# Three small-tile sums and one branch moved in a four-layer graph kernel

## The chip, the cores and the metric
One core of one Trainium2 chip runs the whole program. The metric is device microseconds of one execution; lower is better. Before the change: 2198.82 us, the median of 3 runs (2195.28 to 2202.48).

## The reference
2708 nodes with 256 features pass through four layers; each layer is an attention over an adjacency matrix (`gnn`) and then a feed-forward part (`ffn`), both added to x. Three of the eight parts are touched:

```python
# layer 0 ffn: soft assignment of every node to 64 slices per head, 8 heads
sw = softmax((xm @ W_slice.T + b_slice) / temp)       # 2708 x 512
st = einsum(fx, sw) / (sw.sum + 1e-5); ot = hydra(st) # small
x  = x + einsum(ot, sw) @ out_w.T + out_b
# layer 1 gnn
x  = x + concat([a @ n / deg, n]) @ weight + bias     # n = layernorm(x)
# layer 2 ffn ("mixture two"): 4 experts, two per node
g  = top-2 softmax of the scores, 0 for the other two experts
x  = x + sum over e of g[:, e] * (gelu(n @ W1[e] + b1[e]) @ W2[e] + b2[e])
```

All of it is float32.

## The kernel before
The 2708 nodes are 21 tiles of 128 and one of 20 (`NT` is 22), grouped in `CHUNKS`: five of 512 columns and one of 148, which is a tile of 128 and the tile of 20. Everything stays in the on-chip memory between layers; adjacency and weights stream in. The text is written in program order, and a scheduler then interleaves independent parts on each engine. A `tc.If(...)` block keeps its body together: each of the five engines reads the flag into a register (a tensor load), compares, and jumps over the body when the flag is zero. The scheduler may place instructions that stand outside the block before or behind it: TensorE does the first transposes of unit 0, written after `rare`, ahead of the branch, and SyncE does the flag reads of all three blocks one after the other.

**Slices** (`fast_l0_ffn`, L2481 to L2541). For each tile t TensorE forms the logits `lg` from two products (kk = 0, 1) that accumulate in one PSUM tile (L2482); VectorE adds the bias out of PSUM (L2494), takes a maximum per head (L2495), subtracts (L2496); ScalarE takes the exponential (L2499); VectorE sums (L2500), inverts (L2501) and multiplies (L2502). Then TensorE adds the tile into the four sums `T` (L2508) and transposes it (L2515). After the small middle part, four products accumulate in `po` for each tile (L2533), and VectorE adds `po` to x (L2541).

**Projections** (`fast_l1_gnn`). For each chunk the normalized rows are transposed (`ft_ps`, L1650), and each tile takes four products: two accumulate in `v`, two in `own` (L2605). ScalarE rounds `v` to the high part of V (L2613), VectorE forms the low part (L2614) and adds `own` to x (L2617). The 20 rows of the last tile are then copied by GpSimd's queue to four places (`Vf`, L1588). Behind these copies in the same queue stand the adjacency loads `at` (L2569, 256 KB each); eight buffers of them are filled ahead. The loop over the 21 full source tiles follows (L2646).

**Mixture two** (`fast_l2_ffn`). Expert 0 runs over all chunks and writes to `first` (`park`). `deal.rank` then makes lists of the nodes that use experts 1 and 2; GpSimd gathers these rows (L4581) into `xe`, of which three sets fit. `last_used` sets a flag, whether any node uses expert 3; here none does. Eight units follow, (chunk c, expert i) in turn: `turn` transposes the gathered rows (L4814) through one PSUM tile `xt_ps` in two groups (kk), each copied out by VectorE or ScalarE (L100, L101) before the next may start; `up` multiplies (L4650) and takes the gelu (L4657); `down` multiplies again (L4669), and VectorE adds the bias (L4859) before GpSimd scatters the rows (L4595). Chunk 0 and the last chunk of 148 nodes run plainly for experts 1 and 2 (`expert`, `add`: L4686, L4784), interleaved at the end with `steps`, the first part of layer 3's attention (L3744, L3781). `rare` (L4798) is the block with the branch, for expert 3: it stands once before the units, once after unit 1 and once after unit 2.

Where a tile has only 20 rows, `down` already uses another form: the four products of the sum go to four separate groups of 32 columns of TensorE's array (`y[32 * q : ...]`), each one started and stopped alone, and VectorE adds the four parts (`summed`, L4686 and L4688). It does so for every expert:

```python
g = 1 if n > 32 else 4
```

Of the kernel before, what the change touches and what calls it, by code (L numbers as in the profile page):

```python
# [2450 lines left out]
def fast_l0_ffn(k, w, front):  # L2451

    nc, tc = k.nc, k.tc
    ident = k.ident
    H, P, G = 8, 64, 64
    DI = H * P
    with ExitStack() as ctx:
        keep = ctx.enter_context(tc.tile_pool(name="b0", bufs=1))  # L2460
        swT = keep.tile([128, 4, N], F32, name="swT")
        Tn = keep.tile([128, 4, D + 1], F32, name="Tn")
        Z = keep.tile([128, 4, D], F32, name="Z")
        slices = Slices(k, w, ctx)
        fa, fT, wc, bw = front.fa, front.fT, front.wc, front.bw

        with tc.tile_pool(name="b0t", bufs=3) as tmp:
            with tc.tile_pool(name="ps_b0l", bufs=2, space=PSUM) as psl, tc.tile_pool(
                name="ps_b0T", bufs=1, space=PSUM
            ) as psT:  # L2470

                def psum():
                    return psl.tile([128, 512], F32, name="swt_ps")

                side = front.chunk(*CHUNKS[-1], psum)
                T = [psT.tile([128, D + 1], F32, name=f"T{q}_ps") for q in range(4)]
                for t in range(NT):
                    p = sz(t)
                    next(side, None)
                    lg = psl.tile([128, DI], F32, name="lg_ps")  # L2480
                    for kk in range(2):  # L2481
                        nc.tensor.matmul(  # L2482
                            lg[:p],
                            lhsT=fT[:, kk, t * 128 : t * 128 + p],
                            rhs=wc[:, kk, :],
                            start=(kk == 0),
                            stop=(kk == 1),
                        )
                    xt = k.x[:p, t, :]
                    nc.gpsimd.tensor_tensor(xt, xt, slices.ob[:p], ALU.add)  # L2490
                    sw = tmp.tile([128, DI], F32, name="sw")
                    mx = tmp.tile([128, H], F32, name="mx")
                    s3 = sw[:p].rearrange("p (h g) -> p h g", h=H)
                    nc.vector.tensor_tensor(sw[:p], lg[:p], bw[:p], ALU.add)  # L2494
                    nc.vector.tensor_reduce(mx[:p], s3, AX.X, ALU.max)  # L2495
                    nc.vector.tensor_tensor(  # L2496
                        s3, s3, mx[:p, :, None].to_broadcast([p, H, G]), ALU.subtract
                    )
                    nc.scalar.activation(sw[:p], sw[:p], AF.Exp)  # L2499
                    nc.vector.tensor_reduce(mx[:p], s3, AX.X, ALU.add)  # L2500
                    nc.vector.reciprocal(mx[:p], mx[:p])  # L2501
                    nc.vector.tensor_tensor(  # L2502
                        s3, s3, mx[:p, :, None].to_broadcast([p, H, G]), ALU.mult
                    )
                    tp = psum().rearrange("p (q n) -> p q n", q=4)
                    for q in range(4):
                        cols = slice(q * 128, (q + 1) * 128)
                        nc.tensor.matmul(  # L2508
                            T[q],
                            lhsT=sw[:p, cols],  # L2510
                            rhs=fa[:p, t, :],
                            start=(t == 0),
                            stop=(t == NT - 1),
                        )
                        end = nc.tensor.transpose(tp[:, q, :p], sw[:p, cols], ident[:p, :p])  # L2515
                    nc.scalar.copy(swT[:, :, t * 128 : t * 128 + p], tp[:, :, :p])
                k.busy(psl.tile([128, DI], F32, name="lg_ps"), 6, end)
                for q in range(4):
                    sc = tmp.tile([128, 1], F32, name="sc")
                    nc.vector.tensor_scalar(sc, T[q][:, D : D + 1], 1e-5, None, ALU.add)  # L2520
                    nc.vector.reciprocal(sc, sc)
                    if q < 3:
                        nc.scalar.activation(Tn[:, q, :], T[q], AF.Copy, scale=sc)
                    else:
                        nc.vector.tensor_scalar(Tn[:, q, :], T[q], sc, None, ALU.mult)

        slices.mix(Tn, Z)
        with tc.tile_pool(name="ps_b0o", bufs=3, space=PSUM) as ps:
            for t in range(NT):
                p = sz(t)  # L2530
                po = ps.tile([128, D], F32, name="o_ps")
                for q in range(4):
                    nc.tensor.matmul(  # L2533
                        po[:p],
                        lhsT=swT[:, q, t * 128 : t * 128 + p],
                        rhs=Z[:, q, :],
                        start=(q == 0),
                        stop=(q == 3),
                    )
                xt = k.x[:p, t, :]  # L2540
                nc.vector.tensor_tensor(xt, xt, po[:p], ALU.add)  # L2541


def fast_l1_gnn(k, adjT, weight, bias, order, after, other):
# [6 lines left out]
    with ExitStack() as ctx:  # L2551
# [25 lines left out]
        with tc.tile_pool(name="a1f", bufs=1) as pf, tc.tile_pool(  # L2577
            name="a1t", bufs=3
        ) as tmp, tc.tile_pool(name="a1c", bufs=2) as two, tc.tile_pool(
            name="ps_a1v", bufs=4, space=PSUM  # L2580
        ) as psv, tc.tile_pool(name="ps_ft", bufs=3, space=PSUM) as psf:
            w = pf.tile([128, 4, D], F32, name="w")
            nc.sync.dma_start(w, weight.rearrange("(k p) d -> p k d", p=128))
            b = pf.tile([128, D], F32, name="b")
            nc.sync.dma_start(b, brow(bias, D))

            for c0, cs in CHUNKS:
                bl = blocks(c0, cs)
                t0 = bl[0][0]
                fa = two.tile([128, 4, D], F32, name="fa")  # L2590
                fT = two.tile([128, 2, 512], F32, name="fT")
                for _ in k.norm_chunk(two, fa, t0, len(bl)):
                    pass
                k.transposed(
                    fa,
                    bl,
                    lambda: psf.tile([128, 512], F32, name="ft_ps"),
                    lambda kk: fT[:, kk, :cs],
                    t0,
                )  # L2600
                for t, c, p in bl:
                    v, own = [psv.tile([128, D], F32, name="v_ps") for _ in range(2)]
                    for half, o in enumerate((v, own)):
                        for kk in range(2):
                            nc.tensor.matmul(  # L2605
                                o[:p],
                                lhsT=fT[:, kk, c : c + p],
                                rhs=w[:, half * 2 + kk, :],
                                start=(kk == 0),
                                stop=(kk == 1),  # L2610
                            )
                    hi, lo = V[:p, t, :D], V[:p, t, D + 2 :]
                    nc.scalar.copy(hi, v[:p])  # L2613
                    nc.vector.tensor_tensor(lo, v[:p], hi.bitcast(F32), ALU.subtract)  # L2614
                    xt = k.x[:p, t, :]
                    nc.gpsimd.tensor_tensor(xt, xt, b[:p], ALU.add)
                    nc.vector.tensor_tensor(xt, xt, own[:p], ALU.add)  # L2617
# [1987 lines left out]
def fast_l2_ffn(k, w, edges, deal, then):  # L4605
# [7 lines left out]
    with ExitStack() as ctx:  # L4613
# [48 lines left out]
        def down(e, hT, bl, use):  # L4662
            for t, o, n in bl:
                y = ps2.tile([128, D], F32, name="y_ps")
                g = 1 if n > 32 else 4
                for m in range(M // g):
                    for q in range(g):
                        mq = m + q * M // g
# [15 lines left out]

        def summed(dst, y, n, e):
            done = nc.vector.tensor_tensor(dst, y[:n], b2[:n, e, :], ALU.add)  # L4686
            for q in range(1, 1 if n > 32 else 4):
                done = nc.vector.tensor_tensor(  # L4688
                    dst, dst, y[32 * q : 32 * q + n], ALU.add
                )  # L4690
            return done
# [105 lines left out]
        def rare(chunks):  # L4797
            with tc.If(nc.values_load(flag, min_val=0, max_val=1)):  # L4798
                for c0, cs in chunks:
                    expert(E - 1, c0, cs, add(E - 1))  # L4800

        rare(deal.C[:2])
        steps = then()
        pst = ctx.enter_context(tc.tile_pool(name="ps_mt", bufs=1, space=PSUM))
        zp = ctx.enter_context(tc.tile_pool(name="mz", bufs=2))
# [41 lines left out]
        for u, (c, i) in enumerate(units):  # L4847
# [14 lines left out]

            down(1 + i, hT, [(s, s * 128, 128) for s in range(deal.T[i])], use)
            xT = xT_next
            if u == 1:
                rare(deal.C[2:])
            if u == 2:
# [756 lines left out]
```

## Time and profile before
| what | value |
|---|---|
| runs | 2202.48, 2198.82, 2195.28 us |
| profiled execution, its own time | 2216.88 us |
| its span, first to last instruction | 2215.1 us |
| TensorE busy, matmul / weight load | 2124.0 us (96%) / 1455.6 us (66%) |
| VectorE, ScalarE, GpSimd busy | 1471.3, 887.0, 487.8 us |
| mean granted TensorE clock | 0.987 |
| slices, logits | 374 to 472 us |
| slices, output sums | 507 to 545 us |
| projections | 547 to 589 us |
| mixture two | about 1345 to 1606 us |

The profiled execution is 18.06 us longer than the median of the runs. In the profile PE is TensorE's matmul, PEld its weight load, DVE VectorE, ACT ScalarE, POOL GpSimd, SP SyncE; a `q` behind the name is that engine's instruction queue. Views by line give the time, the length, the instructions and, in brackets, how long the engine sat idle before it and what released it. A float32 product is two records on PE ("passes"), each with its own weight load.

### The profile page before, as it was taken

The numbers are of one execution on the slowest core, as the hardware profiler recorded it, in microseconds if no ns is written. First come the engines' busy times: TensorE is split into PE (matmuls) and PEld (weight loads), VectorE is DVE, ScalarE is ACT, GpSimd is POOL, SyncE is SP. The second block draws the span as 40 slices with busy tenths as digits, with TensorE's granted clock in tenths as the row PEclk, the third lists the DMA queues.
The fourth block names the chain that finished last, engine by engine and source line by source line (L and its number), as shares of the span: only waits on it lengthen the run. The fifth ranks groups of instructions, "written<-read, shape, count | busy, mean of one in ns | idle before, by whom it ended". The sixth has DMA issues, their size and how long they took to land. (4 is left out here: it accounts for less than half of the span.)

```text
span 2215.1 us, 31872 instructions
## 1 busy us (share of the span) xinstructions
PE 2124.0 (96%) x11415; PEld 1455.6 (66%) x11415; DVE 1471.3 (66%) x3190; ACT 887.0 (40%) x1798; POOL 487.8 (22%) x565
## 2 busy tenths in 40 slices
PE   9999999999999999999999999989999999999995
PEld 5766665557899677777678886657743333337784
DVE  7478887866596476755765655554678887885553
ACT  7655665231211322212251003223577777752221
POOL 3100002412354334665400010224110000003321
PEclk9999999999999999999999999999999999999998
DMA  5244432121399334243345554013133434335540
GB/s 163 59 113 115 115 87 90 38 81 47 109 252 257 96 72 122 55 96 79 58 152 144 149 168 117 13 44 97 43 83 105 115 96 116 106 106 165 166 140 14
DMA packets 164164, 234.87 MB, mean 106 GB/s; under 512 B 28556, under 2 KB 97522, under 8 KB 163987
## 3 DMA queue, kind: packets, MB, share of 16 engines
q1 hardware_dynamic: 110616, 156.09, 24.5%
q0 software_dynamic: 35712, 61.71, 11.2%
q10 hardware_dynamic: 17658, 14.81, 2.0%
q8 instruction: 99, 1.62, 0.3%
q14 instruction: 79, 0.64, 0.1%
HBM read 200.27 MB, written 32.77 MB: 105 GB/s over the span
## 5 line engine op out<-in xcount | busy, mean ns | idle before, releaser
L4068 PE MATMUL acc_ps<-PU,V 128*64 128x512 f32 (+5 forms) x1512 | 309.4, 547 | 0.4 <-DVE PU L3910 0.4
L3898 ACT ACTIVATE PU<-Rr,iQ 128x512 f32<-128x512 f32 (+2 forms) x378 | 222.1, 663 | 48.3 <-PE acc_ps L4068 47.4
L3860 DVE SCALAR_TENSOR_TENSOR PT<-Rr,Q,aj 128x512 f32<-128x512 f32 (+3 forms) x252 | 169.7, 683 | 99.1 <-PE acc_ps L3989 68.5
L4068 PE MATMUL acc_ps<-PT,V 128*64 128x512 f32 (+5 forms) x504 | 222.5, 549 | 0.1
L1910 PE MATMUL acc_ps<-fa,PT 128*128 128x257 f32 x882 | 215.6, 383 | 2.5 <-ACT out L1930 1.3
L1910 PEld LDWEIGHTS acc_ps<-fa,PT 128*128 128x128 f32 x882 | 163.7, 190 | 68.9 <-issue 36.2
L3910 DVE SCALAR_TENSOR_TENSOR PU<-PU,aj 128x1536 f32<-128x1536 f32 (+2 forms) x126 | 195.3, 1561 | 6.8 <-ACT PU L3898 6.7
L3989 PE MATMUL acc_ps<-V,PT 128*128 128x257 f32 x882 | 193.8, 381 | 0.0
L3989 PEld LDWEIGHTS acc_ps<-V,PT 128*128 128x128 f32 x882 | 166.3, 190 | 26.0 <-DVE PT L3860 0.8
L3476 PE MATMUL y_ps<-w2t,hT 128*128 128x256 f32 (+1 forms) x784 | 162.7, 387 | 4.1 <-PEq L3654 3.7
L3458 PE MATMUL h_ps<-xT,w1t 128*128 128x384 f32 (+2 forms) x544 | 163.4, 457 | 1.9 <-ACT hT L3465 1.3
L3476 PEld LDWEIGHTS y_ps<-w2t,hT 128*128 128x128 f32 (+1 forms) x784 | 132.4, 182 | 28.9 <-issue 6.4
L4068 PEld LDWEIGHTS acc_ps<-PU,V 128*64 128x64 f32 (+1 forms) x1512 | 91.4, 122 | 83.6 <-issue 72.0
L3465 ACT ACTIVATE hT<-h_ps,b1t 128x384 f32<-128x384 f32 (+2 forms) x136 | 73.2, 539 | 165.1 <-PE h_ps L3458 163.0
L3458 PEld LDWEIGHTS h_ps<-xT,w1t 128*128 128x128 f32 x544 | 101.9, 195 | 54.9 <-ACT hT L3465 3.2
L4068 PEld LDWEIGHTS acc_ps<-PT,V 128*64 128x64 f32 (+1 forms) x504 | 53.3, 122 | 115.9 <-issue 109.6
L2646 PE MATMUL acc_ps<-V,at 128*128 128x258 f32 (+3 forms) x924 | 120.1, 286 | 2.2 <-DMA at<-in_adjT 1.1
L1854 PE MATMUL s_ps<-KT,QT 128*128 128x512 f32 (+1 forms) x252 | 116.4, 549 | 2.5 <-POOL KT L1816 1.4
L1879 DVE SCALAR_TENSOR_TENSOR PT<-aj,PT 128x512 f32<-128x512 int32 (+1 forms) x126 | 79.8, 638 | 55.7 <-ACT PT L1878 55.5
L1834 ACT ACTIVATE junk<-aj,mhalf 128x512 bf16<-128x512 int32 (+1 forms) x126 | 84.3, 669 | 80.0 <-DMA aj<-in_adjT 79.2
L2646 PEld LDWEIGHTS acc_ps<-V,at 128*128 128x128 f32 (+1 forms) x924 | 112.0, 185 | 6.2 <-DMA at<-in_adjT 2.1
L3505 POOL DMA_INDIRECT acc<-ys,ids x45 | 92.9, 2064 | 101.0 <-DVE no L3652 28.8
(908 smaller groups left out, 3757.3 us busy)
## 6 DMA issues: line engine op xcount, KB each, us to landing
aj<-in_adjT SPq DMA_DIRECT2D x294, 256.0 KB
at<-in_adjT POOLq DMA_DIRECT2D x105, 256.0 KB
w1t<-in_L_ffn_W SPq DMA_DIRECT2D x8, 1024.0 KB
w2t<-in_L_ffn_W SPq DMA_DIRECT2D x8, 1024.0 KB
w1t<-in_L_ffn_w SPq DMA_DIRECT2D x8, 1024.0 KB
w2t<-in_L_ffn_w SPq DMA_DIRECT2D x8, 1024.0 KB
fd<-fa ACTq DMA_DIRECT2D x11, 512.0 KB
aj<-in_adjT SPq DMA_DIRECT2D x21, 202.0 KB
```

The costliest lines, as they stand in the source:

```text
L1834: nc.scalar.activation(junk, src, AF.Square, bias=k.mhalf, accum_out=dst)
L1854: nc.tensor.matmul(s[:, :cs], lhsT=QT[:, j * 128 : j * 128 + 128], rhs=KT[:, c0 : c0 + cs], start=True, stop=True,)
L1910: nc.tensor.matmul(ac, lhsT=PT[:, o : o + n], rhs=fa[:, j, :], start=j == 0, stop=False)
L2646: nc.tensor.matmul(ac[:n, :c], lhsT=at[:, o : o + n], rhs=V[:, j, r], start=j == 0 and q == 0, stop=False, skip_group_check=True,)
L3458: nc.tensor.matmul(hp, lhsT=w1t[:, kk, m * 128 : (m + 1) * 128], rhs=self.xT[:, kk, cs], start=(kk == 0), stop=(kk == 1),)
L3476: self.end = nc.tensor.matmul(y, lhsT=self.hT[:, m, i * 128 + p.start : i * 128 + p.stop], rhs=w2t[:, m, :], start=(m == ms[0]), stop=(m = ...
L3505: return nc.gpsimd.indirect_dma_start(out=acc, out_offset=bass.IndirectOffsetOnAxis(ap=self.ids[p, i : i + 1], axis=0), in_=ys[p], in_offs ...
L3860: nc.vector.scalar_tensor_tensor(PT, R, Q, aj, ALU.max, ALU.mult)
L3898: nc.scalar.activation(PU[:, h - 1, :cs], Rr[:, h, c0 : c0 + cs], AF.Copy, scale=front.iQ[:, h, j : j + 1],)
L3910: nc.vector.scalar_tensor_tensor(u, u, 1.0, m, ALU.max, ALU.mult)
L3989: nc.tensor.matmul(ac[:n], lhsT=PT[:, o : o + n], rhs=V[:, j, 0, :], start=(j == 0), stop=False,)
L4068: nc.tensor.matmul(w.pop("out"), **w)
```

## The change
- **Slices, logits**: where a tile has at most 64 rows, the two products go to two groups of 64 columns, and VectorE adds the second part with one more instruction.
- **Slices, output**: where a tile has at most 32 rows, the four products go to four groups of 32 columns; VectorE adds four parts to x instead of one.
- **Projections**: the same for the four products of the 20-row tile, all in `v`; ScalarE copies two parts and VectorE adds two parts, into a spare half of `fa`, before the old instructions follow.
- **Mixture two**: the form with four groups is kept for expert 0 alone; experts 1, 2 and 3 accumulate the 20-row tile in one place, and its three further additions go.
- **The branch**: the first `rare` moves from before the units to behind the first unit (c = 0, expert 1).

```diff
 # fast_l0_ffn
+                    few = p <= 64
                     for kk in range(2):
+                        g = 64 * kk if few else 0
                         nc.tensor.matmul(
-                            lg[:p],
+                            lg[g : g + p],
...
-                            start=(kk == 0),
-                            stop=(kk == 1),
+                            start=few or kk == 0,
+                            stop=few or kk == 1,
...
+                    if few:
+                        nc.vector.tensor_tensor(sw[:p], sw[:p], lg[64 : 64 + p], ALU.add)
...
+                few = p <= 32
                 for q in range(4):
+                    g = 32 * q if few else 0
                     nc.tensor.matmul(
-                        po[:p],
+                        po[g : g + p],
...
-                nc.vector.tensor_tensor(xt, xt, po[:p], ALU.add)
+                for q in range(4 if few else 1):
+                    nc.vector.tensor_tensor(xt, xt, po[32 * q : 32 * q + p], ALU.add)
 # fast_l1_gnn
+                    few = p <= 32
                     for half, o in enumerate((v, own)):
                         for kk in range(2):
+                            g = 64 * half + 32 * kk if few else 0
                             nc.tensor.matmul(
-                                o[:p],
+                                (v if few else o)[g : g + p],
...
+                    if few:
+                        sums = fa[:, 2:4, :]
+                        for half in range(2):
+                            g = 64 * half
+                            nc.scalar.copy(sums[:p, half, :], v[g : g + p])
+                            nc.vector.tensor_tensor(
+                                sums[:p, half, :],
+                                sums[:p, half, :],
+                                v[g + 32 : g + 32 + p],
+                                ALU.add,
+                            )
+                        v, own = sums[:, 0, :], sums[:, 1, :]
 # fast_l2_ffn
-                g = 1 if n > 32 else 4
+                g = 4 if n <= 32 and e == 0 else 1
...
-            for q in range(1, 1 if n > 32 else 4):
+            for q in range(1, 4 if n <= 32 and e == 0 else 1):
...
-        rare(deal.C[:2])
         steps = then()
...
             xT = xT_next
+            if u == 0:
+                rare(deal.C[:2])
             if u == 1:
                 rare(deal.C[2:])
```

More of the change, by code (lines that the diff above doesn't have):

```diff
@@ L2531, in fast_l0_ffn @@
                 po = ps.tile([128, D], F32, name="o_ps")
+                few = p <= 32
                 for q in range(4):
+                    g = 32 * q if few else 0
                     nc.tensor.matmul(
-                        po[:p],
+                        po[g : g + p],
                         lhsT=swT[:, q, t * 128 : t * 128 + p],
                         rhs=Z[:, q, :],
-                        start=(q == 0),
-                        stop=(q == 3),
+                        start=few or q == 0,
+                        stop=few or q == 3,
+                        **(dict(skip_group_check=True) if few else {}),
                     )
                 xt = k.x[:p, t, :]
-                nc.vector.tensor_tensor(xt, xt, po[:p], ALU.add)
+                for q in range(4 if few else 1):
+                    nc.vector.tensor_tensor(xt, xt, po[32 * q : 32 * q + p], ALU.add)
 def fast_l1_gnn(k, adjT, weight, bias, order, after, other):
@@ L2602, in fast_l1_gnn @@
                     v, own = [psv.tile([128, D], F32, name="v_ps") for _ in range(2)]
+                    few = p <= 32
                     for half, o in enumerate((v, own)):
                         for kk in range(2):
+                            g = 64 * half + 32 * kk if few else 0
                             nc.tensor.matmul(
-                                o[:p],
+                                (v if few else o)[g : g + p],
                                 lhsT=fT[:, kk, c : c + p],
                                 rhs=w[:, half * 2 + kk, :],
-                                start=(kk == 0),
-                                stop=(kk == 1),
-                            )
+                                start=few or kk == 0,
+                                stop=few or kk == 1,
+                                **(dict(skip_group_check=True) if few else {}),
+                            )
+                    if few:
[10 more added lines that the diff above has]
+                        v, own = sums[:, 0, :], sums[:, 1, :]
                     hi, lo = V[:p, t, :D], V[:p, t, D + 2 :]
```

## The prediction, on record before the run
> **What bounds the kernel now.** I read the busy shares first, then the idle time of PE stage by stage, then the list of events around each edit.
>
> ```profile
> PE 2124.0 (96%) x11415; PEld 1455.6 (66%) x11415; DVE 1471.3 (66%) x3190; ACT 887.0 (40%) x1798; POOL 487.8 (22%) x565
> ```
>
> PE works 96% of the span, and the other engines are far from full. So an edit pays if it shortens PE's passes, or closes one of PE's gaps. All of PE's gaps together are 68.8 us by the trace. The largest lies in mixture two, at the first flag branch. Windows of 10 us there (columns: PE, PEld, DVE, ACT, POOL with their instruction counts, then granted clock, DMA share, GB/s):
>
> ```profile
> 1470.00:1480.00 10.00, 7.14 (x47) 5.52 (x46) 5.17 (x30) 0.00 (x0) 6.64 (x7) 1.00 0.28 74
> 1480.00:1490.00 10.00, 6.04 (x12) 3.50 (x13) 4.15 (x10) 1.06 (x2) 3.75 (x4) 0.66 0.22 62
> 1490.00:1500.00 10.00, 10.00 (x46) 7.99 (x46) 1.70 (x4) 2.62 (x6) 4.01 (x4) 1.00 0.18 52
> ```
>
> The middle window has a quarter of the passes and a granted clock of 0.66. PE's own list says why:
>
> ```profile
> 1477.03 0.65 PE L4814 MATMUL xt_ps<-ident,xe 128*128 128x128 f32 x3
> 1483.96 0.90 PE L4814 MATMUL xt_ps<-ident,xe 128*128 128x128 f32 x3 [6.28 <-DVE xT L100]
> 1484.69 7.88 PE L4650 MATMUL h_ps<-xT,w1t 128*128 128x384 f32 x16
> ...
> 1505.67 0.38 PE L4814 MATMUL xt_ps<-ident,xe 128*128 128x128 f32 x2
> 1506.69 0.44 PE L4814 MATMUL xt_ps<-ident,xe 128*128 128x128 f32 x2 [0.63 <-DVE xT L100]
> 1507.63 0.55 PE L4814 MATMUL xt_ps<-ident,xe 128*128 128x128 f32 x3 [0.51 <-ACT xT L101]
> 1508.56 5.40 PE L4650 MATMUL h_ps<-xT,w1t 128*128 128x384 f32 x16 [0.38 <-issue]
> ```
>
> PE is idle for 6.28 us, then runs at half clock: the 16 passes of unit 0 take 7.88 us, the same 16 of a later unit 5.40.
>
> **The branch.** What the stall costs now: 6.28 idle, 7.88 − 5.40 = 2.48 slow products, 0.90 − 0.49 = 0.41 slow transposes (0.49 is a group of three at 1501.49). Together 9.17 us. The other two branches stand at small gaps: 0.63 + 0.51 + 0.38 = 1.52, and 0.57 + 0.46 = 1.03 (at 1519.5). Sum 11.72.
>
> What is in the gap? DVE's next step waits as long:
>
> ```profile
> 1483.02 0.42 DVE L4686 TENSOR_TENSOR y<-y_ps,b 128x256 f32<-128x256 f32 x1 [6.04 <-remote]
> ```
>
> The last product before the gap began at 1476.81 and ended by the model near 1477.0, but its signal came at 1482.99, and so did those of the three transposes; elsewhere such signals come about 0.01 us after the end. PE executed its branch at 1478.39 to 1478.71, and its next queue entry came at 1483.12, 4.41 us on; behind eleven other compare-branches of PE the next comes 0.06 us on. So three things meet: PE's first jump over a body, signals held back for 6 us, and the end of a burst of eight gathers on POOL, the last of which is issued here and lands near 1483:
>
> ```profile
> 1480.63 1.00 POOL L4581 DMA_INDIRECT xe<-fd,d_idg  x1 [0.30 <-issue]
> ```
>
> The edit puts the jump behind unit 0. In the built order of the changed kernel PE does six transposes, the products of unit 0 (5.40 us), the transposes of unit 1 and 12 passes of `y`, and only then the branch; POOL has passed all its gathers of the burst, two scatters and two more gathers; DVE and ACT have made their copies; SP's order is unchanged, its three flag reads still stand together. If the stall belongs to the jump meeting work in flight, it goes. What is late next: unit 0 needs both transpose groups through the one bank `xt_ps`, which later units show at 0.57 (wait for the copy) and 0.30 (first product). Unit 1's transposes now come in three pairs of hand-overs rather than two (2 × 0.57 + 0.42 = 1.56), and the branches behind units 1 and 2 keep about 0.99 each. Sum 0.87 + 1.56 + 1.98 = 4.41, so 11.72 − 4.41 = **−7.3 us**. Nothing else is queued behind the moved branch that PE needs within those 12 passes: unit 1's gathers stand ahead of it on POOL, its weights are in the on-chip memory. Bounds: stall wholly gone −7.3; stall stays and the moved jump adds its own, +7 (rival C).
>
> The row says 4.41 us behind this jump and 0.06 behind others. The Trainium skill, "Runtime: NRT & Kernel Launch", section "Instruction fetch mechanics", says that a taken branch to code outside the two fetched pages waits for a DMA fetch of the target. It speaks against the edit: the jump is moved, not removed, and by that rule its 4.41 would move along and this part would be −7.3 + 4.41 = −2.9 at best. No row tells whether these 4.41 are such a fetch.
>
> **Experts 1 and 2, the 20-row tile.** The eight passes in four groups take 0.65 us (1595.64 to 1596.30); one after the other, at 0.216 each (the eight of the slices' last tile take 1.83 in all), 1.73: PE +1.08 for expert 1. For expert 2 the passes are already spread over other products in pairs of 0.6, about 1.8 in all: 0. What goes are six additions on DVE (by lines, with min, median and max ns):
>
> ```profile
> L4688 DVE TENSOR_TENSOR ys<-ys,y_ps x6: 413/416/421, 1598.3 to 1607.5; 20x256 f32<-20x256 f32 x6
> ```
>
> Three of these end the chain of layer 2 into layer 3: `ys` at 1604.41, the additions until 1607.88, the normalization (1.22 us), PE's transposes at 1611.30. PE's own gaps there:
>
> ```profile
> 1607.48 2.05 PE L3744 MATMUL v_ps<-w,fT 128*128 128x264 f32 x8 [1.13 <-DVE fs L3750]
> ...
> 1611.30 0.66 PE L3781 MATMUL v_ps<-ident,fa 128*128 128x128 f32 x4 [1.33 <-DVE fs L3750]
> ```
>
> These gaps of 1.13 and 1.33, and 0.95 at 1599.4, can shrink by at most 2.5 (six times 0.416), less the 1.08. But in the built order expert 2's last passes now stand behind eight passes of `v`, so the chain starts later. I take **−0.6**; bounds −2.5 to +1.1.
>
> **Slices, logits.** PE saves two passes in parallel, 2 × 0.43 = 0.86, but here DVE is the bound (PE waits 0.43, 0.70 and 0.80 us for it between 460 and 467). DVE starts one every 0.60 us:
>
> ```profile
> 463.68 0.67 DVE L2494 TENSOR_TENSOR sw<-lg_ps,bw 20x512 f32<-20x512 f32 x1
> ...
> 467.50 0.68 DVE L2500 TENSOR_REDUCE mx<-sw 20x8 f32<-20x512 f32 x1 [0.52 <-ACT sw L2499]
> ```
>
> One more of these is 0.60, and the built order puts a 128-row product ahead of the small tile's subtraction, which delays the last exponential by 0.60 more: **+1.2**; bounds −0.86 to +1.3.
>
> **Slices, output.** Eight passes over the 20 columns take 1.83 us now (543.03 to 544.86); in four groups 0.65, the duration of the same shape in mixture two. The three more additions lie beside the transposes of layer 1. **−1.2**; the other end, if three additions of 0.416 come on the path, is +0.1.
>
> **Projections.** Eight passes, 8 × 0.216 = 1.73 against 0.65: −1.1. Given back: two ACT copies (0.36 each) and two additions (0.42 each) stand between the product and V's rows, whose four copies are ahead of the adjacency loads on POOL:
>
> ```profile
> 592.48 1.68 POOL L2569 DMA_DIRECT2D at<-in_adjT  x3
> ```
>
> They delay this by 2 × (0.36 + 0.42) = 1.56 at most. PE takes 0.95 us per source tile and has eight loads ahead, so a late issue is felt only where DMA is the bound, and its share is near 1.0 between 590 and 720. I take 0.5 of it (between ends 0 and 2.3, near the first, since PE never waits for these loads in its first tiles): **−0.6** for this part.
>
> Sum: −7.3 − 0.6 + 1.2 − 1.2 − 0.6 = **−8.5 us**. From the profiled 2216.88 that gives 2208.4; the median of the runs lies 18.06 lower, so 2198.82 − 8.5 = **2190.3**.
>
> **Rivals.** About 0.3%, 6.6 us, is what a measurement of this kernel can tell from no change: the bounds are 2192.2 and 2205.4.
>
> A: the stall isn't the jump's. The trace shows smaller held-back signals of PE near other long runs of gathers (1.7 us at 775, 1.36 at 2026), and none of these has a flag branch. Then unit 0 meets the same burst, since POOL's gathers stay where they are, or the stall is there only in the profiled execution. The branch part gives 0 to +1.0 (a third hand-over, 0.57 + 0.42), in the middle +0.7; the others −0.6 + 1.2 − 1.2 − 0.6 = −1.2: together −0.5, **2198.3**. For it: the four signals are those of passes that ended before PE read its flag. Against it: the burst began at 1471.5, and PE ran unharmed for six of its gathers; and POOL's own queue had no fault.
>
> C, the slower side: the burst's stall stays, and the jump at its new place pays for itself. Place: PE's queue behind the 12 passes of `y`. Price: 4.41 idle (1478.71 to 1483.12) and 2.48 + 0.41 at half clock behind it, since PE has no queued work past the branch. It decides as soon as the idle time before unit 0 does not shrink by more than 0.5. Total −0.5 + 4.41 + 2.89 = +6.8: **2205.6**. For it: the half clock came with the gap, and the gap came with the jump's next entry. Against: branches two and three, 1506 and 1519, jump over bodies too and cost 1.5 and 1.0, hand-overs included.
>
> The cost of the half clock is a row here: 2.48 + 0.41. The Trainium skill, "TensorE: Matmul & The Clock Gate", section "What's actually happening", gives an idle window of about 3.4 us for the drop, and as long at work for the return; by that a gap cut below 3.4 us would save the whole 2.9, and an estimate from its figures for the return is at most 3.4. The row shows 0.5 from 1482.88 to 1489.7, 6.8 us.
>
> **How the numbers follow.** Forecast B (stall goes) 0.45, A 0.40, C 0.15. B for the branches two and three, which show that a jump of all five engines need not cost 6 us. B's own range, by the unknown terms −2.5 + 1.1 and ±2, is 2187 to 2193; A's 2195 to 2202, as wide as the three runs of before; C's 2203 to 2208. The range from 2187 to 2203 leaves out C and some of the edges, 2 in 10. Faster 0.45, same 0.40, slower 0.15.
>
> **What would show it.** B right: no PE gap over 1.5 us between 1465 and 1530, granted clock 1.0 throughout, 5.40 us for unit 0's 16 passes. A: a gap of 4 to 6 us ahead of unit 0, none behind the 12 passes. C: both. The parts: 0.65 us for the eight passes of the slices' output and of the projections; a wait of DVE near 1.1 before the last sum of the slices; the first load L2569 at about 1 us later against the first product of its stage; the gap before layer 3's first transposes below 1.33. It is wrong if DMA near 600 was the bound after all, or if another gap of PE over 3 us arises where POOL or SP now stand differently.

## The result and the profile after

| | median of 22 runs, us | span of the profiled execution |
|---|---|---|
| before | 2198.49 (2195.28 to 2202.53) | 2215.1 |
| changed | 2202.22 (2196.79 to 2206.77) | 2204.7 |

The ratio is 1.0017, 95% interval 1.0009 to 1.0024: the change made the kernel 2.0 to 5.3 us slower. The forecast was 8.5 us faster, with slower given a chance of 0.15. The two profiles point the other way (10.4 us shorter). The profile of before is of an execution of 2216.88 us, which none of its 22 runs reaches (at most 2202.53); the experiments below show what it holds that they do not.

PE's work on the page is 6.7 us less than before, its share the same:

```profile
PE 2117.3 (96%) x11415; PEld 1454.6 (66%) x11415; DVE 1474.6 (67%) x3190; ACT 887.9 (40%) x1800; POOL 488.4 (22%) x565
```

PE's list of the changed kernel around the moved branch (start, length, operation, and in brackets the idle time before it and what ended it):

```profile
1475.11 0.55 PE L4836 MATMUL xt_ps<-ident,xe 128*128 128x128 f32 x3 [0.65 <-DVE xT L100]
1475.81 5.40 PE L4673 MATMUL h_ps<-xT,w1t 128*128 128x384 f32 x16
...
1486.66 0.49 PE L4836 MATMUL xt_ps<-ident,xe 128*128 128x128 f32 x3
1487.86 0.55 PE L4836 MATMUL xt_ps<-ident,xe 128*128 128x128 f32 x3 [0.71 <-DVE xT L100]
1489.02 0.44 PE L4836 MATMUL xt_ps<-ident,xe 128*128 128x128 f32 x2 [0.61 <-ACT xT L101]
1490.60 5.21 PE L4673 MATMUL h_ps<-xT,w1t 128*128 128x256 f32 x16 [1.15 <-PEq L4821]
```

The 6.28 us stall is not there and unit 0 runs at 5.40. But around the branch's new place three hand-overs stand bare (PE has no other work to fill them), 2.47 us, and the 16 products behind it take 5.21 us, where the same shape takes 3.69 at a later unit: half clock again. The window shows it in the granted clock (the column behind POOL):

```profile
1490.00:1500.00 10.00, 8.93 (x35) 7.42 (x35) 1.50 (x4) 2.26 (x5) 5.41 (x6) 0.83 0.25 81
```

The second loss is where the forecast had none, behind the slices' output. PE, then DVE, then POOL of the changed kernel:

```profile
549.09 0.63 PE L1650 MATMUL ft_ps<-ident,fa 128*128 128x128 f32 x4 [1.37 <-DVE fa L1688]
549.55 3.62 PE L2615 MATMUL v_ps<-w,fT 128*128 128x256 f32 x16
556.31 0.91 PE L2615 MATMUL v_ps<-w,fT 128*128 128x256 f32 x3 [3.13 <-DVE V L2637]
```

```profile
549.32 5.18 DVE L1688 TENSOR_SCALAR fa<-x,ln_rs,ln_sh 128x256 f32<-128x256 f32 x3
```

```profile
550.12 4.23 POOL L2639 TENSOR_TENSOR x<-x,b 128x256 f32<-128x256 f32 x6
```

Three normalizations that take 0.41 us each elsewhere take 5.18 together, two of them 2.59 and 2.17, while GpSimd does six bias additions without a break. VectorE's next work on `v` (the low part, L2637) stands behind them, and PE waits 3.13 us.

To put a price on each stage I take the start of the same PE instruction in two traces and see by how much the difference grows over a stage. The partners are the experiments that leave the stage as it was and whose chip has none of the stalls (`logits_only`; for the logits `tail_only`).

| stage | forecast, us | difference grown, us |
|---|---|---|
| slices, logits (455 to 475) | +1.2 | +0.72 |
| slices, output and what follows (505 to 565) | −1.2 | +3.75 |
| projections (565 to 700) | −0.6 | +0.07 (+1.0 against `tail_only`) |
| branch (1455 to 1515) | −7.3 | +3.16 |
| tail (1570 to 1618) | −0.6 | −0.82 |

The sum is +6.9, above the runs' 2.0 to 5.3. Two of the terms change from execution to execution, as the experiments show, and this is one execution; its 2206.47 us lie 4.25 above the median of its own runs.

### The profile page after: what moved, and what is told of

Its sections match the earlier page's. It is cut to its first block, busy times and chain, and to the rows that moved or that the text cites. A ratio compares the mean times of both kernels' runs of the same rounds, so it can differ in the third digit from the quotient of the medians.

```text
span 2204.7 us, 31877 instructions
## 1 busy us (share of the span) xinstructions
PE 2117.3 (96%) x11415; PEld 1454.6 (66%) x11415; DVE 1474.6 (67%) x3190; ACT 887.9 (40%) x1800; POOL 488.4 (22%) x565
## 3 DMA queue, kind: packets, MB, share of 16 engines
q1 hardware_dynamic: 110616, 156.09, 24.3%
```

## The experiments

The experiments ran on five chips. One (`branch_only`, `branch_left_out`, `tail_only`, `logits_only`) ran the kernel before in 2196.42 us; the four others in 2219 to 2224: one with the four runs on the output and the projections, one with `branch_again`, `branch_held`, `combined` and `output_nobias_all`, one with `control`, `rares_left_out`, `gathers_two` and `after_mended`, one with `late_flag` and `combined_late`. So ratios are read against before on the same chip, and traces of the two sorts are not mixed for a price.

### Is it the moved branch?

`branch_only` is before with the diff's last two hunks alone. `branch_left_out` has no first block at all:

```diff
-        rare(deal.C[:2])
         steps = then()
```

> The kernel before with the first branch moved behind the first unit and nothing else. Forecast B: 7.3 us faster. Rival A (the 9 us stall is in the profiled execution only, or belongs to the gathers): -1 to +1 in the runs, while the profile may show a stall or not. Rival C: 7 us slower.

> The kernel before without the first block for expert 3, branch and body, which no node uses; the other two blocks stay. If the branch makes the stall and the stall is in the runs too: 7 to 9 us faster. Rival A: 0 to -1 us in the runs; if the gathers make the stall, it still stands near 1478 in the profile, if the branch does, the profile has none.

Measured: 1.0004 (0.9993 to 1.0015) and 1.0008 (0.9998 to 1.0018). Leaving the branch out brings nothing in the runs of this chip, and moving it does not bring 7 us. The reason is in the trace of `tail_only`, same chip, with the branch at its old place. PE there:

```profile
1466.91 0.52 PE L4814 MATMUL xt_ps<-ident,xe 128*128 128x128 f32 x3 [1.19 <-PEq L4798]
1467.65 5.40 PE L4650 MATMUL h_ps<-xT,w1t 128*128 128x384 f32 x16 [0.22 <-DMA xe<-fd,d_idg]
```

The same code passes the same branch with 1.19 us idle and at full clock. The stall of 6.28 us is not on every chip. None of the four traces of this chip has it; on three of the slower chips all traces with SyncE's flag reads beside eight gathers have 5.95 to 6.44 us. The first profile, by its stall and its 2216.88 us, looks like those, and the runs of before (2198) like the faster chip. That they were on different chips is inferred: the record does not name them. In `branch_only` the moved branch has the same hand-overs as in the changed kernel: idle times of 0.70, 0.61 and 1.11, and then

```profile
1483.99 6.68 PE L4650 MATMUL h_ps<-xT,w1t 128*128 128x256 f32 x16 [1.11 <-PEq L4798]
```

Its trace grows by 4.46 us in this stage against `tail_only`; its runs say −1.5 to +3.3. The half clock is not the same in every execution (6.68 us for the 16 products here, 5.21 in the changed kernel); how often it comes in the runs stays open.

The same kernel on a chip that stalls, and a version in which the transposes don't stand bare:

```diff
+            hT, last = up(1 + i, lambda kk: xT[:, kk, :n], n)
             if u + 1 < len(units):
-                xT_next = turn(*units[u + 1])
+                with tc.issue_after(last.ins) if u in (1, 2) else nullcontext():
+                    xT_next = turn(*units[u + 1])
```

> branch_only once more, on another chip if it falls so. Where the kernel before stalls 6.3 us at its first branch: forecast B gives -5 to -7 us, rival A 0. Where it does not: +1 to +4.5 us by branch_only's trace.

> As branch_only, but the transposes of units 2 and 3 are held until the products of the unit before are issued, so that none stands bare in front of a branch. Theory 2 (the moved branch costs by bare hand-overs through the one bank, 0.70 + 0.61 + 1.11, and the half clock that follows them, 1.5 to 3.1): no product of unit 1 at half clock, the stage 3 to 5 us shorter than in branch_only, and -1 to -3 us against before. Rival (the jump itself costs): the gap at the branch and the slow products stay.

Measured: `branch_again` 1.0001 (0.9989 to 1.0013), `branch_held` 1.0006 (0.9992 to 1.0019). PE in `branch_again`:

```profile
1482.41 0.90 PE L4813 MATMUL xt_ps<-ident,xe 128*128 128x128 f32 x3 [5.97 <-DVE xT L100]
1483.10 7.26 PE L4650 MATMUL h_ps<-xT,w1t 128*128 128x384 f32 x16
...
1499.80 5.38 PE L4650 MATMUL h_ps<-xT,w1t 128*128 128x256 f32 x16 [1.18 <-PEq L4798]
```

This is the blow to forecast B: PE's jump now stands at 1499, and the stall is still ahead of unit 0. So the jump does not make it. In `branch_held` unit 1's products are back at full speed with no idle time before them that the list shows:

```profile
1495.35 3.69 PE L4650 MATMUL h_ps<-xT,w1t 128*128 128x256 f32 x16
```

Its stage is 5.8 us shorter than that of `branch_again` (difference of growth, 1455 to 1515, same chip), of which 1.5 is lost by 1535, where the branch behind unit 2 has bare transposes again. The cause of the stage's loss is shown: bare hand-overs, then half clock. That the runs gain by it is not: the two ratios are the same within their intervals.

### What makes the stall?

`control` is before, unchanged. `rares_left_out` drops all three blocks. `gathers_two` has two sets of gathered rows:

```diff
-        xp = ctx.enter_context(tc.tile_pool(name="mx", bufs=3))
+        xp = ctx.enter_context(tc.tile_pool(name="mx", bufs=2))
...
-                for i in range((2, 1, 0, 0)[c]):
+                for i in range((2, 0, 0, 0)[c]):
...
-            if u + 3 < len(units):
-                xes[units[u + 3]] = gathered(*units[u + 3])
+            if u + 2 < len(units):
+                xes[units[u + 2]] = gathered(*units[u + 2])
```

> The kernel before, unchanged, on the same chip: shows whether this chip has the stall near 1478 (6.28 us in the first profile) and what the flag reads of SyncE take.

> The kernel before without any of the three blocks for expert 3, flag reads and branches included. On a chip whose unchanged kernel stalls about 6 us near 1478: if the flag reads or the branch make the stall, it is gone and the time falls 7 to 9 us, and 2 more for the hand-overs at the other two; if the gathers make it, 4 to 6 us of it stay. On a chip without the stall: -1 to -3 us.

> The kernel before with two sets of gathered rows in place of three, so that five gathers and not eight stand ahead of the first branch. On a chip with the stall: if the gathers make it, the idle time before unit 0's second transposes is under 3 us; if the flag reads or the branch do, 5 to 6 us stay. Time against before open, -5 to +5, since later gathers come closer to their use.

PE before unit 0's second transposes, in `control`, `rares_left_out` (with the products that follow) and `gathers_two`:

```profile
1482.30 0.90 PE L4814 MATMUL xt_ps<-ident,xe 128*128 128x128 f32 x3 [6.37 <-DVE xT L100]
```

```profile
1476.91 0.55 PE L4813 MATMUL xt_ps<-ident,xe 128*128 128x128 f32 x3 [0.65 <-DVE used L4399]
1477.44 7.09 PE L4650 MATMUL h_ps<-xT,w1t 128*128 128x384 f32 x16
```

```profile
1478.37 0.55 PE L4814 MATMUL xt_ps<-ident,xe 128*128 128x128 f32 x3 [2.15 <-DVE xT L100]
```

Without the blocks the stall is gone (1.63 us of waiting for a gather stand ahead of the first transposes), though the eight gathers stay, and the time falls: 0.9961 (0.9947 to 0.9975), 8.7 us. Against `control`, 6.6 us of it arise between 1455 and 1515. The slow products are not won: unit 0's 16 take 7.09 us here and 7.17 in `control`, where full clock is 5.40. With five gathers ahead the stall shrinks to 2.15, and the time is 0.9985 (0.9971 to 0.9998), though a later gather now comes 2.75 us late (PE at 1504.13). So the 6 us take both: the flag reads, or something else of these blocks' entry, and gathers in flight; and they need a chip of this sort. A row of gathers alone stops PE there too, for less: `control` has 2.34 us idle at 1395.64 and `rares_left_out` 2.32 at 1394.21, both among GpSimd's gathers with no flag read near, where `tail_only` has none. SyncE's reads are what `branch_again` leaves in place. Their steps by line, on the chip without the stall (`tail_only`) and in `control` (min, median, max in ns):

```profile
L4798 SPq SEQ_ASSERT  x3: 18/18/18, 1464.4 to 1465.6; - x3
```

```profile
L4798 SPq SEQ_ASSERT  x3: 13/726/737, 1476.2 to 1480.5; - x3
```

A step of 18 ns takes 0.73 us. One of the three is as slow in `gathers_two`, where PE waits 2.15 us. Whether SyncE's reads make the stall or suffer it with the rest was not told apart, nor why chips differ.

`late_flag` keeps the computation whole: the flag is computed behind unit 0, and one block behind unit 2 stands for the three.

> The kernel before with the flag computed behind unit 0, and one block for expert 3 behind unit 2 in place of three; no read of the flag meets the first row of gathers. If the stall needs flag reads and gathers together: on a chip with the stall no idle time over 2 us near 1478 and 7 to 9 us faster, as with the blocks left out; on a chip without it 0 to -2 us. If the gathers alone make it, 4 to 6 us idle stay.

Measured: 0.9999 (0.9984 to 1.0014), a miss in time and a hit in place. No trace of before was taken on this chip; its 2219.13 us make it one of the slower sort. The idle time ahead of unit 0 is 1.52 us, but the one branch now costs:

```profile
1512.23 6.21 PE L4652 MATMUL h_ps<-xT,w1t 128*128 128x256 f32 x16 [5.33 <-PEq L4799]
```

```profile
L4799 PEldq COMPARE_BRANCH  x1: 4379/4379/4379, 1507.7 to 1507.7; - x1
```

The jump itself takes 4.38 us; the moved one took 0.35 in the changed kernel, with two chunks in its body where this one has six. The 16 products behind it take 6.21 where full clock is 3.69. Against `control`, on another chip of the slower sort, about 9 us are won by 1515 and all given back by 1535.

### Which part of the sums loses?

`output_only` is the output's hunk alone. `output_nobias` leaves out GpSimd's bias additions for the first eight tiles, `output_nobias_all` for all. `output_first` turns the loop:

```diff
-            for t in range(NT):
+            for t in [NT - 1, *range(NT - 1)]:
                 p = sz(t)
                 po = ps.tile([128, D], F32, name="o_ps")
```

> The kernel before with the slices' output sums of the 20-row tile in four groups and nothing else. Theory 1 (the added additions turn VectorE's order, so that two normalizations meet a row of GpSimd additions on one port): the two stretched normalizations of 2.2 to 2.6 us and a PE gap of about 3 us near 553 are there; 3 to 5 us slower than before in the runs. The forecast's step (the additions lie beside transposes): 1.2 us faster. Rival (the loss of the change comes from the moved branch or the profile only): between -1.2 and 0.

> As output_only, but GpSimd's bias additions of layer 1 are left out for the first eight tiles (so x lacks the bias there); VectorE's order of instructions stays. Theory 1: the normalizations go back to about 0.41 us each, the gap near 553 shrinks from 3.1 to under 1, and the time is 2.5 to 4 us below output_only. Rival (only the order counts, or they wait for something else): the normalizations stay over 2 us and the time equals output_only.

> As output_only, but all of layer 1's bias additions on GpSimd are left out (x lacks that bias). The earlier cut left eight additions just where they met the normalizations. Theory 1 (one port between VectorE and GpSimd additions): no normalization of this stage over 0.7 us, no PE gap over 1.6 us between 545 and 565. Rival (the order of VectorE's work alone): a normalization over 2 us or a gap over 3 us stays.

> As output_only, but the 20-row tile is the first of the output sums, not the last, so its three further additions fall where VectorE has 0.6 us free per tile. Theory 1: no stretched normalization, 8 passes in 0.65 us, about 1.2 us faster than before (0 to -2). Rival (four groups cost PE or VectorE time wherever they stand): slower than before.

Measured: `output_only` 1.0008 (0.9994 to 1.0022), `output_nobias` 1.0021 (1.0004 to 1.0038), `output_first` 0.9999 (0.9987 to 1.0011); of `output_nobias_all` there is one execution, the profiled one. The normalizations of this stage by line (number, then min, median and max in ns), in the order changed kernel, `output_only`, `output_nobias`, `output_nobias_all`, `output_first`:

```profile
L1688 DVE TENSOR_SCALAR fa<-x,ln_rs,ln_sh x4: 395/1374/2590, 548.5 to 552.3; 128x256 f32<-128x256 f32 x4
```

```profile
L1688 DVE TENSOR_SCALAR fa<-x,ln_rs,ln_sh x6: 553/816/948, 546.3 to 564.3; 128x256 f32<-128x256 f32 x6
```

```profile
L1688 DVE TENSOR_SCALAR fa<-x,ln_rs,ln_sh x4: 395/604/3904, 549.2 to 551.1; 128x256 f32<-128x256 f32 x4
```

```profile
L1688 DVE TENSOR_SCALAR fa<-x,ln_rs,ln_sh x6: 389/400/411, 545.5 to 562.4; 128x256 f32<-128x256 f32 x6
```

```profile
L1688 DVE TENSOR_SCALAR fa<-x,ln_rs,ln_sh x6: 402/406/437, 547.3 to 563.4; 128x256 f32<-128x256 f32 x6
```

`output_nobias` went against my expectation: one normalization took 3.90 us. It keeps the additions of the later tiles, and GpSimd did eight of them in one row at 551.33 to 556.92, over that normalization. With all additions out, none is over 0.41 and PE has no gap over 1.4 us there. With the additions in but the order unturned (`output_first`), none is over 0.44. So for the stretched rows the mechanism is shown: both are needed, VectorE's turned order and GpSimd's row of additions. The turned order alone already takes back what the groups save: in `output_nobias_all` the stage is 0.3 us behind `control` (a chip of the same sort), with PE waiting 1.37 us for a normalization, while in `output_first` it is 1.4 ahead. What the meeting adds is a draw: in `output_only` the two engines took turns (0.55 to 0.95 each) and the stage lost 0.8 against `control`, in the changed kernel 3.75, in `output_nobias` 6.3. No run's time tells `output_only` or `output_first` from before.

### The other parts, and versions

> The kernel before with the projections of the 20-row tile in four groups and nothing else. The forecast's step: 0.6 us faster (8 passes saved 1.1, 0.5 given back). Reading of the changed kernel's trace (the stage gains 0.9 on PE, but its first product stands 1.98 us idle against 0.62): 0.5 to 1 us slower.

> The kernel before with the 20-row tile of experts 1 to 3 in one accumulation and nothing else. Forecast: -0.6 us; by the changed kernel's trace -0.9. Bounds -2.5 to +1.1.

> The kernel before with the slices' logits of the 20-row tile in two groups and nothing else. Forecast +1.2 us; by the changed kernel's trace +0.7. Bounds -0.86 to +1.3.

Measured: 1.0011 (0.9993 to 1.0028), 0.9994 (0.9985 to 1.0003), 1.0006 (0.9993 to 1.0019). None is told from nothing by its runs. Added to `branch_only` and `output_only` they make +0.23%, near the changed kernel's +0.17%, but over two sorts of chip. By the stages the tail gains 0.8 and the logits lose 0.7, both within the bounds given. In `proj_only` and in the changed kernel PE's first product of layer 1 waits 1.98 us in place of 0.62: the copies and additions ahead of V eat the passes saved. The stage's price depends on the partner (−0.3 to +1.0 for the changed kernel over the four traces of the faster chip), so its sign stays open.

`combined` has the tail's change, the output and the projections with the 20-row tile first, the transposes ahead of the second and third branch held, and nothing else. `after_mended` is the changed kernel with `output_first`'s loop and `branch_held`'s hold. `combined_late` is `combined` with `late_flag`.

> The kernel before with the tail's change, the output sums and the projections in four groups with the 20-row tile first in each, the transposes ahead of the second and third branch held, the first branch at its old place, the logits as before. By the stages: tail -0.8, output -1.4, projections -1 to -1.5, held transposes -1.5: 4 to 6 us faster than before. Rival (what the stages gain is lost later or in the spread): -2 to +1.

> The changed kernel with two things mended: the 20-row tile is the first of the output sums, and the transposes of units 2 and 3 are held behind the products of the unit before. Theory (the change loses by the turned order with the port, about 3.7 in its trace, and by bare hand-overs with half clock, 3.2): 1 to 4 us faster than before, against 3.7 us slower of the change. Rival (the loss lies in the four-group forms or the jump): still 2 to 4 us slower than before.

> late_flag with what combined has: the tail's change, output sums and projections in four groups with the 20-row tile first, transposes ahead of the branch held. By the stages 3 to 4 us faster than late_flag: -10 to -12 us against before on a chip with the stall, -4 to -6 without. Rival (the small gains are lost again, as in combined): equal to late_flag.

Measured: `combined` 0.9993 (0.9980 to 1.0006), `after_mended` 1.0001 (0.9988 to 1.0015), `combined_late` 0.9982 (0.9965 to 0.9998). `after_mended` lies 0.16% below the changed kernel's 1.0017, on another chip and with intervals that touch; that fits with the two mechanisms but leaves no gain over before. `combined_late` is, with `gathers_two`, the only version with the whole computation that beats before, by 0.4 to 7.8 us, on a chip of the slower sort; both intervals only just clear 1. The held transposes and the jump's 4.29 us overlap there, so that 2.58 us of idle time are left. The gains expected of the three (4 to 6, 1 to 4 and 10 to 12 us) did not come: what the stages gain does not add up in the runs.

## Why the prediction was wrong

The measured 2202.22 lies just inside the range, 2187 to 2203, but by luck: the sum pointed to 2190.3, and the time moved the other way.

**The branch.** The step that failed is "If the stall belongs to the jump meeting work in flight, it goes." The jump went and the stall stayed (5.97 us in `branch_again`). Nor were the 4.41 us behind the first jump the jump's: in `tail_only` the next entry of PE's queue comes 0.06 us behind the same jump at the same place, and in `branch_again` 0.12 behind the moved one. The text had the facts against it: the held-back signals were of passes that ended before PE read its flag, and "SP's order is unchanged, its three flag reads still stand together". It priced them at nothing. One fact that it used for rival A was wrong: it says that none of the smaller hold-ups at 775 and 2026 has a flag branch, but PE passes one near both (L3654 at 772.94, L5341 at 2026.80), with gaps of 1.34 us at 775.85 and 1.73 at 2025.15. So these could not tell the jump from the gathers.

**The basis.** A second step failed with it: "the median of the runs lies 18.06 lower, so 2198.82 − 8.5". About 7.5 of the profile's extra 18 us arise at the stall itself (1455 to 1515, against `tail_only` and `logits_only`). A saving that exists only in the execution that is slower must not be taken off the runs that are faster. Rival A said so ("only in the profiled execution") and was right on this part: the runs moved by none of the 7.3. On the faster chip there is no stall to remove: the same place has 1.19 us in `tail_only`. Nor was the price right where the stall exists: of the 2.48 us for slow products, 1.69 stayed in `rares_left_out` without it (7.09 against 5.40).

**The branch's new place.** The forecast counted the hand-overs (1.56 us) but gave them to unit 1's transposes. By their numbers (three, three, two) the ones that stand there are unit 2's and the first of unit 3's, drawn ahead of the branch. Nor did it count what they do to the clock: 2.47 us idle within 4 us, and the next 16 products took 1.5 to 3.1 us more. Rival C had the right sign and the half clock, by a wrong mechanism: the jump itself took 0.35 us, not 4.41.

**The output sums.** "The three more additions lie beside the transposes of layer 1" failed. The PE passes were saved as said (the difference shrinks by 1.3 us up to 546). But the additions stood among VectorE's copies and normalizations, the scheduler put the next chunk's two normalizations ahead of the work on `v`, and these met GpSimd's additions. The built order, which I had, shows the first half: four additions of 20 rows between the copies, then three normalizations in a row. I had bounded the step at +0.1 by the additions' own length; +3.75 came from what they displaced.

**Logits, projections, tail.** The terms +1.2, −0.6 and −0.6 measured about +0.7, −0.3 to +1.0, and −0.8. In the projections the give-back was taken at 0.5 and was 0.8 to 2.1. For the logits, two of the three waits that the text gives to VectorE (0.43 and 0.70) were released by ScalarE in the trace.

The Trainium skill, "SBUF — State Buffer", section "Who interferes with whom", says that VectorE's `tensor_scalar` can need a port pair that GpSimd also uses, and that the later one blocks for the whole instruction; the stretched rows agree (0.41 to 2.59 and 3.90 us), and also show that a row of GpSimd additions can keep VectorE out over several of them.

The rule on code fetch that the forecast weighed, from the Trainium skill's "Runtime: NRT & Kernel Launch", section "Instruction fetch mechanics", fits `late_flag`: the jump over six chunks takes 4.38 us, over two 0.35. The size of the body was not varied by itself, so the fetch is argued, not shown. The forecast's own 4.41 us were no such fetch, since the same jump has 0.06 in `tail_only`.

## What to carry to other kernels

Compare the profiled execution with the runs before pricing a stall: if it is slower by more than the stall, look for the stall in a second profile first. An instruction added to an engine off the critical path is priced by the order that it turns, not by its length: read the built order of that engine for what now stands ahead of PE's next need, and GpSimd's list for what runs at that time. A fixed point such as a branch leaves the work that the scheduler draws ahead of it bare; let that work wait for the products of the step before.

## What the runs showed of the hardware

- Chips differ by 1.2% on the same program (2196.42 against 2222.77 us), and the traces place most of it: `control` falls 24.3 us behind `tail_only`, 4.3 of them between 1380 and 1400, 6.9 between 1455 and 1515 and 6.3 between 2000 and 2020 (times of `tail_only`). At each of the three GpSimd issues gathers one behind the other; at the first no flag is read.
- TensorE's clock falls to a half without one long gap: 0.70 + 0.61 + 1.11 us of idle time between short transposes was enough for 6.68 us in place of 3.6 to 3.7. The granted clock is then 0.5 for 6.8 us, in the changed kernel for 3.4. The Trainium skill, "TensorE: Matmul & The Clock Gate", section "What's actually happening", gives one idle window of about 3.4 us; the measured gaps, none over 1.2, decide here.
- PE's jump over two chunks of work takes 0.32 to 0.36 us in `control` and in the changed kernel, one over six 4.38 in `late_flag` and 4.29 in `combined_late`.
